# Four-layer cross-attention model: batches in pairs become a running sequence half the layers apart, and GpSimd adds two key tiles of probabilities before the sums

## Chip, cores and metric

One NeuronCore of one Trainium2 chip runs the whole program. The metric is the device time of the kernel in microseconds (us), as the median of several runs; lower is better. Engine names as the profile has them: PE is TensorE (PEld its weight loads), DVE is VectorE, ACT is ScalarE, POOL is GpSimd, SP is SyncE, which here only issues DMAs. PSUM is the memory that TensorE writes, SBUF the working memory.

## The reference, cut to what matters

The input is x (16 batches, 256 tokens, 128 channels) and a context ctx (16 batches, 1601 rows, 64 channels). Four layers follow each other, and each is an attention and a feed-forward part:

```python
x = x + L0_xattn(ln(x), ctx)   # causal self-attention + cross-attention, 16 heads of 8
x = x + L0_ffn(ln(x))          # top 4 of 32 hashed experts
x = x + L1_xattn(ln(x), ctx)   # cross-attention, 16 heads of 8
x = x + L1_ffn(ln(x))          # quantised, with a convolution over channels
x = x + L2_xattn(ln(x), ctx)   # self-attention, ffn, then cross-attention, ffn; 16 heads of 32
x = x + L2_ffn(ln(x))          # top 1 of 8 experts
x = x + L3_xattn(ln(x), ctx)   # cross-attention, 16 heads of 8
x = x + L3_ffn(ln(x))          # top 2 of 16 experts and a shared one
```

Batches are independent of each other. Within one batch every line needs the one above it. Each cross-attention is softmax(q k^T) v of 256 queries over 1601 keys in 16 heads. The "third attention" of the change is the cross-attention inside L2.

## The kernel before

**Work.** A cross-attention is cut into four *slabs* of four heads (`attend`, line 1046). A slab has two parts. First the maxima: 28 products of queries with stretches of keys into PSUM (tile `bank<-k,q`), each followed by a DVE reduction (`mx<-bank`). They give every query's largest score; POOL splits it in three bf16 parts (`thirds`, tile `nmp`), TensorE turns it (`shift_T`, tile `nmT`). Then seven steps over the 13 key tiles, two tiles a step and one in the last, which has 65 rows: transposed scores of four heads (`st_ops`, tiles `st<-q,k` and, for the subtracted maximum, `st<-nmT,ones`), four exponentials on ACT (`exps`, `p<-st`), and the products of probabilities with values and, for heads of 32, with a matrix of ones that gives the softmax's denominators (`weigh`, tiles `bank<-p,v` and `bank<-p,ones`). Four heads lie in four row or column groups of the array. Heads of 8 (L0, L1, L3; "narrow") carry the column of ones inside their values, so they have no products with ones. Heads of 32 (L2; "wide") use plain f32 operands, so a product of queries and keys is two matmul instructions and not one.

The rest of a batch is its *chain*: layer norms, projections, L0's and L2's self-attentions (`own_attention`), feed-forward parts, and for a new batch `load_ctx` (line 754), which loads and normalises the context and transposes it. `queries8`, `parts8` and `keys` for narrow heads spread the heads over the partitions with small DMAs on SP, four per slab (`spread`, line 808, tiles `q<-hl`, `k<-hl`): 16 for a batch's queries, 16 for its keys in each cross-attention, and 32 for L0's self-attention.

**Order.** Nothing is issued as it is written. `Program.record` (line 195) collects units of work, and `emit` (line 341) plans them: it keeps a clock for every engine, and whenever an engine is free takes the ready unit of lowest rank whose buffers are free. The plan's order is the program order of each engine on the chip. The rank is a level (`CHAIN` before `ENDS` before `OWN` before `STEPS`) and inside it a place. Chain work therefore goes first, L0's self-attention later, and the maxima and steps fill what is left, in the order of their places: step j of slab number n stands at n + j/7, its maxima at n - 1 - LEAD and up, with LEAD = 0.4 of a slab. A DMA of SP is planned at `t = 0.07` us of its queue (line 398). Matmuls of successive calls into one PSUM tile form one unit, so all products of a `weigh` are one.

**Buffers.** Each class of tiles has a number of places: 7 for `k` (the keys of a slab, also the context under load), 2 for `v`, 12 for `p`, 6 for `w4` (wide tiles: the queries of a cross-attention, the four tiles of a self-attention, hidden layers), 7 PSUM banks and one accumulator. `k`, `v` and the transposed contexts `ctxT` (2 places) are given out in the order of recording.

**Batches.** The loop at line 1365 takes two batches at a time. Per pair the order of cross-attentions is L0 of the first, L0 of the second, L1 of the first, L1 of the second, and so on. While one batch attends, the other one's chain runs. The context of the next pair is recorded after the whole of this pair.

Of the kernel before, what the change touches and what calls it, by code (L numbers as in the profile page):

```python
# [13 lines left out]
F32R = mybir.dt.float32r  # L14
# [3 lines left out]
ALU = mybir.AluOpType  # L18
# [3 lines left out]
P = 128  # L22
# [26 lines left out]

CHAIN, ENDS, OWN, STEPS = 0, 1, 2, 3  # L50

LEAD = 0.4
NAHEAD = 2


# [396 lines left out]
def model(ctx: ExitStack, tc: tile.TileContext, d, out):  # L452
# [158 lines left out]
    def places(tag, n, **how):  # L611
# [11 lines left out]
        for t, n, how in (  # L623
            ("bank", 7, {"psum": True}), ("acc", 1, {"psum": True, "gang": False}),
            ("k", 7, {"ordered": True}), ("v", 2, {"ordered": True}),
            ("ctxT0", LANES, {"ordered": True}), ("ctxT1", LANES, {"ordered": True}),
            ("p", 12, {}), ("wst", 2, {}), ("w4", 6, {}), ("tok", 10, {}), ("chan", 6, {}), ("chan_r", 3, {}),
            ("vs8", 1, {}), ("y8", 2, {}), ("nmT1", NAHEAD, {}), ("nmT4", 1, {}), ("nm4", 1, {}),
            ("lg32", 1, {}), ("lg8", 1, {}), ("lg17", 1, {}), ("gate32", 1, {}), ("gate8", 1, {}), ("gate17", 1, {}),
            ("bn", 4, {}), ("mv", 4, {}), ("rs", 4, {}), ("cm", 1, {}), ("cr", 1, {}), ("rc8", 4, {}), ("third", 4, {}),  # L630
            ("nm", 4, {}), ("mx", 4, {}), ("m8", 2, {}), ("ix", 2, {}), ("fx1", 2, {}), ("fx2", 2, {}), ("fx4", 2, {}),
            ("rw2", 2, {}), ("rw4", 2, {}), ("sw", 2, {}), ("am", 2, {}), ("sg", 1, {}),
        )
    }
    for tag, ts in (("nmp", nmp[4:]), ("nmp4", nmp[:4])):
# [6 lines left out]
    def new(tag, shape, base, dtype=F32, loose=False):  # L642
        return prog.tile(classes[tag], shape and list(shape), dtype, name(base), loose)
# [7 lines left out]
    def evac(o, i, bias=None):  # L651

        if bias is None:
            nc.scalar.copy(o, i)
        else:
            nc.scalar.activation(o, i, AF.Identity, bias=bias)
# [226 lines left out]
    def accumulators(tag):  # L883
        return bank(tag).rearrange("p (u q) -> p u q", u=2)

    def weigh(att, s, av, pr, t0, n, r, last, sums=True, values=True):


        for i in range(n):
            first, fin = t0 + i == 0, last and i == n - 1  # L890
            if values:
                for g in range(4):
                    mm(av[32 * g : 32 * g + 32, 0, :], att.value(s, t0 + i, g, r), pr[g][:r, i, :],
                       first and (sums or att.d8), fin, True)
            if sums and not att.d8:
                for g in range(4):
                    mm(av[32 * g : 32 * g + 32, 1, :], ones[:r, :32], pr[g][:r, i, :],
                       first and not values, fin, True)

    def normalised(att, s, av):  # L900
        if att.d8:
# [105 lines left out]
                    r = rows_of(t + whole)  # L1007
                    yield t + whole, 1, r, ps2[h][:r, whole * P : m * P]

    def keys(ctxT, l):  # L1010
        ks = {}
        if l == "l2":
            for s in range(4):
                t = new("k", [P, NK], "k32")
                for k0, k1, p in halves(wkv2[:, s * P : (s + 1) * P], ctxT[1], NK):
                    evac(t[:, k0:k1], p)
                ks[s] = t
        else:
            hl = [new("k", [P, NKE], "hl", F32R) for _ in range(2)]
            bias = W.get(l + "_bck")  # L1020
            for k0, k1, p in halves(W[l + "_Wck"], ctxT[0], NKE):
                split([t[:, k0:k1] for t in hl], p, bias)
            for s in range(4):
                t = new("k", [P, NKE], "k8", F32R, loose=True)
                spread(t, hl, s, True)
                ks[s] = t
        return ks

    def values(ctxT, l):
        vs = {}  # L1030
        if l == "l2":
            for s in range(4):
                v = new("v", [P, NT, P], "v32")
                for t, m, r, p in value_tiles(ctxT[1], wkv2[:, 512 + s * P : 512 + (s + 1) * P]):
                    evac(v[:r, t : t + m, :].rearrange("p t e -> p (t e)"), p)
                vs[s] = v
        else:
            v, v9 = values8("v", NT, ctxT[0])
            for t, m, r, p in value_tiles(ctxT[0], W[l + "_Wcv"]):
                evac(v9[:r, t : t + m, :, :8], p.rearrange("p (t h e) -> p t h e", t=m, h=H))  # L1040
            vs[0] = v
        return vs

    slab_no = [0]

    def attend(att):

        steps = [(t, min(2, NT - t), rows_of(t)) for t in range(0, NT, 2)]
        w = NKE if att.d8 else NK
        for s in range(4):  # L1050
            mx = new("mx", [P, 2, 4, 4], "mx", loose=True)
            stretches = [(range(q, q + 1), c * 512, c * 512 + 512) for q in range(2) for c in range(3)]
            stretches.append((range(2), 3 * 512, w))
            n = slab_no[0]
            slab_no[0] += 1
            for i, (qs, k0, k1) in enumerate(stretches):
                for g in range(4):
                    with prog.at(STEPS, n - 1 + (4 * i + g) / (4 * len(stretches)) - LEAD):
                        h = slice(32 * g, 32 * g + 32)
                        m, j = k1 - k0, k0 // 512  # L1060
                        p = bank()[:, : m * len(qs)].rearrange("p (q k) -> p q k", k=m)
                        with prog.together((g,)):
                            for q in qs:
                                mm(p[:, q - qs[0], :], att.q[h, s, q * P : (q + 1) * P], att.k[s][h, k0:k1])
                        nc.vector.tensor_reduce(mx[:, qs[0] : qs[-1] + 1, g, j], p, AX.X, ALU.max)
            with prog.at(ENDS):
                nm = new("nm", [P, 2, 4], "nm")
                nc.vector.tensor_reduce(nm, mx, AX.X, ALU.max, negate=True)
                sh = new("nmp", None, "nmp")
                thirds(sh, nm)  # L1070
                nmT = shift_T([sh])[:, 0, :]
            av = None
            for j, (t0, m, r) in enumerate(steps):
                with prog.at(STEPS, n + j / len(steps)):
                    pr = [exps(att, t, m, r) for t in st_ops(att, s, t0, m, r, nmT)]
                    if av is None:
                        av = accumulators("acc")
                    weigh(att, s, av, pr, t0, m, r, t0 + m == NT)
            with prog.at(ENDS):
                normalised(att, s, av)  # L1080
        return att.o


    def route(logits, n, k, gate):
# [277 lines left out]


    prog.recording = True
    for b0 in range(0, nb, LANES):
        lanes = range(b0, min(nb, b0 + LANES))
        ctxTs, lives = {}, {}
        for b in lanes:
            with prog.at(CHAIN):
                ctxTs[b] = load_ctx(b)  # L1370
                lives[b] = life(b, ctxTs[b])
        atts = {}
        for l in LAYERS:
            for b in lanes:
                with prog.at(CHAIN):
                    if l == "l0":
                        atts[b] = next(lives[b])
                with prog.at(CHAIN):
                    ks = keys(ctxTs[b], l)
                    vs = values(ctxTs[b], l)  # L1380
                atts[b].k, atts[b].v = ks, vs
                attend(atts[b])
                with prog.at(CHAIN):
                    atts[b] = next(lives[b], None)
    with tc.manual_schedule():
        prog.emit()

# [118 lines left out]
```

## Time and profile before

| what | value |
| --- | --- |
| median of 3 runs | 9560.31 us (9547.48 to 9571.74) |
| profiled execution: time, span | 9500.53 us, 9498.8 us |
| PE, DVE, ACT, POOL busy | 93%, 62%, 54%, 11% |
| mean granted TensorE clock | 0.904 |
| chain that ended last, by engine | PE 80%, DVE 8%, ACT 4%, SP's queue 3% |
| products with ones | 7680 instructions, 586.2 us busy |
| DMA | mean 33 GB/s |

The profile is of one execution, with its span counted from the first to the last instruction; its own time is 1.7 us longer. Busy time of PE counts matmuls that stand in its pipeline, so 93% doesn't say that it runs at its peak. The granted clock is a share of TensorE's full clock. All operations go through one helper, so they have one line (L395), and it is tiles that tell them apart.

### The profile page before, as it was taken

What the parts mean: (1) busy time and instruction counts of PE and PEld (TensorE: products, weight loads), DVE (VectorE), ACT (ScalarE), POOL (GpSimd) and SP (SyncE); (2) the same over time, 40 slices, a digit from 0 to 9 for tenths busy, and PEclk for the clock granted to TensorE, in tenths of its full rate; (3) what the DMA queues carried; (4) which work ended last, traced back from release to release, by engine and by line L of the source; (5) the groups of instructions that cost most, each with busy time, mean ns of one, the idle gap of its engine ahead of it and who ended that gap; (6) DMA issues with size and microseconds to landing.
All of it is one profiled execution on the core that took longest, in us unless ns stands there. A gap on an engine that the chain in (4) does not pass through costs nothing.

```text
span 9498.8 us, 210842 instructions
## 1 busy us (share of the span) xinstructions
PE 8874.5 (93%) x86118; PEld 5239.1 (55%) x86118; DVE 5863.8 (62%) x12308; ACT 5171.3 (54%) x10590; POOL 1080.9 (11%) x2747
## 2 busy tenths in 40 slices
PE   6999899998999989999899998999989999899999
PEld 3556555565555655556455564555645556455565
DVE  4755657556675565755667555676566755567555
ACT  2654556555564555645556454664555645566455
POOL 2011110111101011010110101101010010100100
PEclk7989889898898988989899897898988989899898
DMA  2200212002120021200212002120011101111011
GB/s 55 49 18 15 45 37 54 14 14 48 38 52 11 14 49 36 53 11 18 47 39 49 11 18 46 39 49 11 20 45 44 43 11 21 45 45 44 11 22 32
DMA packets 158879, 313.48 MB, mean 33 GB/s; under 512 B 65163, under 2 KB 116275, under 8 KB 157910
## 3 DMA queue, kind: packets, MB, share of 16 engines
q1 hardware_dynamic: 154676, 297.83, 13.6%
q8 instruction: 678, 11.11, 0.5%
q14 instruction: 291, 2.38, 0.1%
q0 software_dynamic: 768, 1.48, 0.0%
q10 hardware_dynamic: 2466, 0.68, 0.0%
HBM read 98.31 MB, written 2.10 MB: 11 GB/s over the span
## 4 chain that ended last, share of the span: by engine, by line
PE 80%; DVE 8%; ACT 4%; SPq 3%; issue 2%; DMA 2%; POOL 1%; ACTq 0%; DVEq 0%; POOLq 0%
PE bank L395 53%; PE st L395 22%; PE mx L395 4%; DVE mx L395 4%; SPq L395 3%; ACT p L395 3%; DMA k<-hl 1%; DVE z L395 1%; DVE x L395 1%; DVE st L395 1%; DMA ws<-in_s_l3f_dram 1%; DVE mv L395 0%; POOL nmp L395 0%; ACT ctxT L395 0%; DVE rc L395 0%
## 5 line engine op out<-in xcount | busy, mean ns | idle before, releaser
L395 DVE TENSOR_REDUCE mx<-bank 128x1 f32<-128x512 f32 (+2 forms) x7168 | 4093.1, 627 | 1967.6 <-PE bank L395 1871.6
L395 ACT ACTIVATE p<-st 128x512 f32<-128x512 f32 (+1 forms) x7680 | 3849.8, 575 | 2460.8 <-PE st L395 2310.6
L395 PE MATMUL st<-q,k 32*128 32x256 f32 (+1 forms) x18176 | 2531.6, 370 | 154.6 <-ACT p L395 105.7
L395 PE MATMUL bank<-k,q 32*128 32x512 f32 (+2 forms) x10240 | 2375.5, 521 | 174.8 <-DVE hl L395 88.6
L395 PEld LDWEIGHTS st<-q,k 32*128 32x128 f32 (+1 forms) x18176 | 1644.3, 190 | 1011.0 <-issue 361.7
L395 PE MATMUL bank<-p,v 128*32 128x256 f32 (+1 forms) x27648 | 2105.8, 412 | 0.0
L395 PE MATMUL st<-nmT,ones 32*128 32x512 bf16 (+1 forms) x7680 | 1682.0, 389 | 0.0
L395 PEld LDWEIGHTS bank<-k,q 32*128 32x128 f32 x10240 | 1042.2, 198 | 740.5 <-ACT p L395 199.5
L395 PEld LDWEIGHTS bank<-p,v 128*32 128x32 f32 (+1 forms) x27648 | 757.6, 114 | 896.6 <-issue 607.5
L395 POOL CAST nmp<-nm 128x8 bf16<-128x8 f32 x384 | 84.4, 220 | 4852.8 <-DVE nm L395 4465.1
L395 PE MATMUL bank<-p,ones 128*32 128x256 f32 (+1 forms) x7680 | 586.2, 384 | 0.0
L395 PEld LDWEIGHTS <-ones 32*128 32x128 bf16 (+1 forms) x7680 | 485.8, 98 | 116.5
L395 DVE TENSOR_REDUCE nm<-mx 128x2 f32<-128x512 f32 (+1 forms) x768 | 378.8, 520 | 253.8 <-PE mx L395 238.0
L395 DVE RECIPROCAL rc<-bank 128x8 f32<-128x8 f32 (+1 forms) x384 | 276.1, 719 | 293.0 <-PE bank L395 287.2
L395 POOL TENSOR_SCALAR_AFFINE_SELECT p<-p 128x512 f32<-128x512 f32 x512 | 300.3, 624 | 701.2 <-PE bank L395 490.0
L395 ACT ACT_TABLE_LOAD x222 | 284.8, 1283 | 149.5 <-PE st L395 108.0
L395 PE MATMUL mx<-k,q 32*128 32x256 f32 x1536 | 305.4, 426 | 63.0 <-DMA k<-hl 42.8
L395 POOL TENSOR_TENSOR rs<-rs,neghalf 128x2 f32<-128x2 f32 x240 | 170.3, 710 | 1663.3 <-DVE rs L395 1648.9
L395 PEld LDWEIGHTS bank<-p,ones 128*32 128x32 f32 (+1 forms) x7680 | 248.5, 111 | 178.0 <-issue 10.6
L395 ACT COPY v<-bank 128x512 f32<-128x512 f32 (+3 forms) x592 | 232.5, 451 | 144.5 <-PE bank L395 143.9
L395 PEld LDWEIGHTS mx<-k,q 32*128 32x128 f32 x1536 | 216.4, 215 | 164.5 <-issue 46.2
L395 PEld LDWEIGHTS bank<-ws,h 128*128 128x128 f32 x1664 | 231.7, 222 | 46.6 <-issue 32.3
(221 smaller groups left out, 6545.0 us busy)
## 6 DMA issues: line engine op xcount, KB each, us to landing
k<-hl SPq DMA_DIRECT2D x768, 200.2 KB, 3.6
q<-hl SPq DMA_DIRECT2D x1024, 32.0 KB, 1.9
ws<-in_s_l_a_li_dram SPq DMA_DIRECT2D x32, 768.0 KB
ws<-in_s_l3f_dram SPq DMA_DIRECT2D x32, 768.0 KB, 7.3
ws<-in_s_l0f_dram SPq DMA_DIRECT2D x32, 512.0 KB, 6.0
ws<-in_s_l_a_qkv_dram SPq DMA_DIRECT2D x16, 768.0 KB, 4.2
k<-hl SPq DMA_DIRECT2D x256, 32.0 KB, 1.9
ws<-in_s_l3f_dram SPq DMA_DIRECT2D x16, 384.0 KB
```

The source lines that it names most:

```text
L395: getattr(getattr(self.nc, e), method)(*a, **k)
```

## The change

**Batches.** The pairs go. One sequence of slabs for all 16 batches is made (`slabs_in_order`), and from the second batch on it repeats: L0 of batch b+1, L2 of batch b, L1 of batch b+1, L3 of batch b. Between L1 and L2 of one batch there now lie two cross-attentions of others (narrow ones), between its other layers one: L2's between L0 and L1, L1's between L2 and L3. A new batch's context is loaded when L3 of the batch two before it begins, and one at a time. The sequence starts with L0, L0, L1, L2 (of the first batch), L1 (of the second), L3 (of the first), and it ends with L1 and L3 of the last two and then L2 and L3 of the last batch alone.

**Places.** Steps and maxima get their places from a running count (`clock`): 18 units for a narrow slab, 34 for a wide one, 18 for a slab's maxima, which end 4 units ahead of its steps or earlier. The keys and values of a wide slab are recorded slab by slab, and a step now also waits for the values (`prog.behind`).

**Sums.** In a wide slab's six steps of two key tiles, POOL adds the two tiles' probabilities of each head (new tiles `ps`, four places), and TensorE multiplies that sum with ones, once and not twice. `p` has 11 places and not 12.

```diff
-LEAD = 0.4
+LONG8, LONG32, LONGM, LEAD = 18, 34, 18, 4
...
-            ("p", 12, {}), ("wst", 2, {}), ("w4", 6, {}), ...
+            ("p", 11, {}), ("wst", 2, {}), ("w4", 6, {}), ... ("ps", 4, {}),
...
-    def weigh(att, s, av, pr, t0, n, r, last, sums=True, values=True):
+    def weigh(att, s, av, pr, t0, n, r, last, sums=True, values=True, both=None):
...
-            if sums and not att.d8:
+            if sums and not att.d8 and both is None:
                 for g in range(4):
                     mm(av[32 * g : 32 * g + 32, 1, :], ones[:r, :32], pr[g][:r, i, :],
                        first and not values, fin, True)
+        if both is not None:
+            for g in range(4):
+                mm(av[32 * g : 32 * g + 32, 1, :], ones[:r, :32], both[g], False, last, True)
...
+    def attend(att, s, begin, ahead):
...
+                with prog.at(STEPS, ahead + (4 * i + g) * LONGM / (4 * len(chunks))):
...
+            with prog.at(STEPS, begin + j * (LONG8 if att.d8 else LONG32) / len(steps)), prog.behind(att.v[0 if att.d8 else s]):
...
+                both = None
+                if m == 2 and not att.d8:
+                    both = [new("ps", [P, T], "ps") for _ in range(4)]
+                    for o, e in zip(both, pr):
+                        nc.gpsimd.tensor_tensor(o, e[:, 0, :], e[:, 1, :], ALU.add)
+                weigh(att, s, av, pr, t0, m, r, t0 + m == NT, both=both)
...
+    def slabs_in_order():
+        def whole(b, l):
+            return [(b, l, s) for s in range(4)] if b < nb else []
+        seq = whole(0, "l0") + whole(1, "l0") + whole(0, "l1")
+        for b in range(nb):
+            x, y = whole(b, "l2"), whole(b + 1, "l0") if b else []
+            if y:
+                seq += y + x
+            else:
+                seq += x
+            seq += whole(b + 1, "l1") + whole(b, "l3")
+        return seq
+
+    def clock(seq):
+        begin, t = [], 0.0
+        for _, l, _ in seq:
+            begin.append(t)
+            t += LONG32 if l == "l2" else LONG8
+        ahead, t = [], 1e9
+        for t0 in reversed(begin):
+            t = min(t, t0 - LEAD) - LONGM
+            ahead.append(t)
+        return list(zip(seq, begin, reversed(ahead)))
...
-    for b0 in range(0, nb, LANES):
-        lanes = range(b0, min(nb, b0 + LANES))
...
+    begun(0)
+    begun(1)
+    for (b, l, s), begin, ahead in clock(slabs_in_order()):
+        att, ctxT = atts[b], ctxTs[b]
+        with prog.at(CHAIN):
+            if l == "l2":
+                att.k[s], att.v[s] = keys32(ctxT, s), val32(ctxT, s)
+            elif s == 0:
+                att.k, att.v[0] = keys8(ctxT, l), val8(ctxT, l)
+        if l == "l3" and s == 0:
+            begun(b + 2)
+        attend(att, s, begin, ahead)
+        if s == 3:
+            with prog.at(CHAIN):
+                atts[b] = next(lives[b], None)
```

`begun(b)` loads a batch's context, starts its chain and runs it up to L0's cross-attention; `keys8`, `val8`, `keys32` and `val32` are the two branches of the old `keys` and `values`.

## The prediction

> **What bounds the kernel now.** I read the page first.
>
> ```profile
> PE 8874.5 (93%) x86118; PEld 5239.1 (55%) x86118; DVE 5863.8 (62%) x12308; ACT 5171.3 (54%) x10590; POOL 1080.9 (11%) x2747
> PEclk7989889898898988989899897898988989899898
> PE 80%; DVE 8%; ACT 4%; SPq 3%; issue 2%; DMA 2%; POOL 1%; ACTq 0%; DVEq 0%; POOLq 0%
> L395 PE MATMUL bank<-p,ones 128*32 128x256 f32 (+1 forms) x7680 | 586.2, 384 | 0.0
> ```
>
> TensorE carries the end: 80% of the last chain, and no other engine near its limit. The clock row shows a dip in every fifth slice or so: a pair of batches lasts about 1180 us, five slices.
>
> So I looked at one pair. The last key tile's products have a form of their own (32x65), so the timeline tells when each slab ends. Cutting at the ends of attentions from 2527 us on gives eight stages: L0 twice, L1 twice, L2 twice, L3 twice (columns: length, then busy us of PE, PEld, DVE, ACT, POOL, then clock and DMA).
>
> ```profile
> 2527.00:2642.00 115.00, 110.55 (x1033) 65.91 (x1028) 79.13 (x165) 71.04 (x145) 4.99 (x20) 0.88 0.21 48
> 2642.00:2741.00 99.00, 94.40 (x998) 55.40 (x993) 77.10 (x165) 67.55 (x144) 6.44 (x22) 0.98 0.23 51
> 2741.00:2851.00 110.00, 105.97 (x1018) 61.17 (x1010) 75.31 (x162) 69.87 (x147) 6.42 (x22) 0.86 0.25 60
> 2851.00:2999.00 148.00, 142.35 (x1247) 80.07 (x1243) 82.10 (x177) 83.21 (x172) 21.18 (x53) 0.84 0.02 7
> 2999.00:3242.00 243.00, 231.08 (x2297) 142.39 (x2297) 138.94 (x286) 105.83 (x209) 28.69 (x69) 0.92 0.04 11
> 3242.00:3390.00 148.00, 146.37 (x1752) 91.31 (x1744) 84.73 (x170) 75.75 (x155) 7.92 (x24) 1.00 0.14 28
> 3390.00:3497.00 107.00, 100.94 (x1037) 59.30 (x1037) 80.98 (x175) 72.38 (x148) 19.73 (x33) 0.94 0.23 47
> 3497.00:3710.00 213.00, 183.79 (x1415) 103.31 (x1411) 113.12 (x238) 101.59 (x210) 37.24 (x96) 0.80 0.17 41
> ```
>
> Undisturbed slabs end 19.6 to 22.5 us apart when narrow (2699, 2719, 2741) and 33.8 us when wide. I take 20.5 and 34: 82 us for a narrow attention, 136 for a wide one. What the stages have over that is the price of the chains: 33, 17, 28, 66, 107, 12, 25, 131, together 419 of 1183 us. Two stages stand out. In the fifth the first wide slab ends only at 3133, 134 us after the stage begins: the first batch's chain of L1's feed-forward and L2's self-attention (from the last `o` at 2858 to the cross-attention's queries at 3020, 162 us) was not hidden by one narrow attention, and the second's then ran beside little else. In the eighth the next pair's two contexts and two L0 self-attentions fall together. There the plan is wrong about SP:
>
> ```profile
> 3521.49 10.75 SPq L395 DMA_DIRECT2D q<-hl  x16
> 3533.44 12.09 SPq L395 DMA_DIRECT2D q<-hl  x16
> 3545.63 10.10 SPq L395 DMA_DIRECT2D k<-hl  x16
> ```
>
> Sixteen small DMAs take 10.1 to 12.1 us to issue, 0.63 to 0.76 each where the plan has 0.07. TensorE, whose order is fixed, stands behind them:
>
> ```profile
> 3529.04 0.79 PE L395 MATMUL bank<-k,q 32*128 32x512 f32 x2 [9.98 <-DVE hl L395]
> 3542.05 1.22 PE L395 MATMUL bank<-zT,w_l_Wq 128*128 128x256 f32 x2 [3.87 <-DVE hl L395]
> 3553.31 0.76 PE L395 MATMUL mx<-k,q 32*128 32x256 f32 x2 [7.15 <-DMA k<-hl]
> ```
>
> That is 21 us of standing in a pair, and the clock after it is 0.50.
>
> **The change, part by part.** I sum against the profiled 9500.5 us, which lies 59.8 below the median of 9560.3.
>
> *Sums.* 64 wide slabs have six steps of two tiles; each loses four f32 products, eight instructions: 3072 of 7680. The timeline prices them in a wide slab:
>
> ```profile
> 3304.86 0.64 PE L395 MATMUL bank<-p,v 128*32 128x256 f32 x8
> 3305.32 0.61 PE L395 MATMUL bank<-p,ones 128*32 128x256 f32 x8
> 3305.75 0.61 PE L395 MATMUL bank<-p,v 128*32 128x256 f32 x8
> ```
>
> From start to start eight take 0.43 us, so 384 x 0.43 = 165 us. Bounds: nothing, if a wide slab waits for something else (its stage has PE busy 146 of 148 at full clock, which speaks against), and 3072 x 586.2/7680 = 234 by the group. I take -165.
>
> *GpSimd.* It gains 1536 additions of 128x256. The nearest row:
>
> ```profile
> L395 POOL TENSOR_TENSOR xb<-x,biases 128x256 f32<-128x256 f32 x96 | 69.7, 734 | 529.3 <-DVE x L395 528.7
> ```
>
> At 0.734 us that is 1127 us more of POOL (11% to about 23%), 2.9 per step of 34/7 = 4.9 us, so it fits beside the step. But the products of a step form one unit, which now waits for the last addition, with the next step's scores and the maxima behind it in TensorE's order, and ACT and DVE waiting for those. The cover is what the plan puts between, scores and maxima of later places, some 3 us a step in this stage; without it each of 384 steps stands for an addition, 384 x 0.734 = 282 us. `p` is held that much longer and has one place less: two steps take eight, so 11 still leave a third begun. And `thirds` (four operations of 0.22) may find an addition running: half of 0.734 at 64 slabs, 24 us. The lead of maxima before a wide slab shrinks from 0.4 of it to 4 of 34 units; later products fill what it opens. The new wait for values costs nothing: they are made a slab ahead. I take +25 for all this; bounds 0 and +282. One rule speaks against the additions: the Trainium skill (Advanced Engine Details and Errata, VectorE Performance Modes) has GpSimd share VectorE's second SBUF port, so that each blocks the other. The trace has 734 ns beside a VectorE mostly reducing from PSUM, and nothing on two-port instructions; were an addition to take twice that, four would need 5.9 us against 4.9, and the sum would be 384 us worse. I go by the row.
>
> *L1 to L2.* This chain now has two narrow attentions over it (164 us bare) and not one. The first batch's cost its stage 66 and the second's 107 over bare. If all cost 66: -41 for each of 8 pairs, -328. Bounds: 0 if 107 is work and not gaps; -66 more per pair if the first's cost halves for both.
>
> *New batch.* 131 in the eighth stage includes an L3 feed-forward, 33 in the first stage, so two loads cost 98, one 49. One at a time beside an L3 attention needs 32 small DMAs for itself and 16 for the queries at once, not 96. The stage lost 21 us of standing and, by clock 0.80, up to 0.2 x 213 = 43 more, 32 per batch. I take 0.6 of it, 19, for 14 batches: -266. Bounds: -32, and +49 (below). What the self-attention's own products do is unclear: the Trainium skill (TensorE: Matmul & The Clock Gate, Part 1) releases the clock after some 3.4 us of sustained activity, yet from 3560 to 3570 PE was busy 10.00 of 10 us at 0.50. By the rule nothing cold would remain beside an attention, and the term would be its full -448; I go by the row.
>
> *L2 to L3.* The first batch of a pair had this beside a wide attention at 12; now all pay 25 beside a narrow one: 13 x 8 = +104. L0's feed-forward goes from 17 and 28 beside narrow attentions to beside a wide one, where the sixth stage's chain cost 12: I take no change.
>
> *Ends.* The first batch's L1 to L2 has no attention over it: 162 - 66 = +96. The last batch's has one: +14. The last L2 to L3 stands open, 53 us (3396.5 to 3449.5) and 17 of maxima, less the 25 counted: +45. Together +155.
>
> Keys and values of wide slabs, recorded slab by slab, keep their cost and their queues; ACT copies and TensorE products are the same in number, and the place of `k` and `v` decided their time before too.
>
> Sum: -165 + 25 - 328 - 266 + 104 + 155 = -475, so 9025.5, and with 59.8 a median of 9085.
>
> **Rivals.**
> *Each load stalls alone (slower).* Place: SP's queue at every L3. The plan keeps 0.07 per DMA, so each batch can make TensorE stand as a pair did: a load costs 98 and not 30. Then +49 x 14 = +686 in the place of -266: 9978, median 10037. It decides from 64 us a load on (475/14 = 34 more than 30). For: the lines above. Against: only 21 of the 98 is standing, and one batch issues half.
> *Chains are work, not gaps (slower).* Neither -328 nor -266 comes: +119, 9619, median 9679. For: PE is busy 231 of 243 in the fifth stage. Against: that stage's 2297 instructions are fewer per us than the sixth's 1752 in 148.
> *The order does not come apart.* `w4` has six places: L3's queries 1, L2's self-attention 4, the new L0's queries 1, and then nothing for its own attention. If a batch waits for places, half of the 594 is lost: 9322, median 9382, faster by the sums and little else.
> *More hides.* With two attentions over it the chain from L1 to L2 costs all batches 33, half of 66: 528 more, less 66 at the two ends: 8563, median 8623.
>
> **Numbers.** Chances: forecast 0.50 (its own range 8900 to 9300), order not apart 0.15, more hides 0.13, loads stall 0.13, work not gaps 0.09. The range may leave out 0.2: the stalled loads and half of the last; 8600 to 9600. A measurement tells 0.3% (29 us) from no change. Faster: 0.50 + 0.15 + 0.13, less 0.02 of the second for no change and 0.01 for slower: 0.75. Slower: 0.13 + 0.09 + 0.01 = 0.23. No change: 0.02.
>
> **What would show it.** Right: `bank<-p,ones` with 4608 instructions; POOL near 2200 us with additions near 734 ns; no first wide slab over 100 us long after an L1, except the first batch's; narrow attentions with a chain beside them between 100 and 150 us, a steady cycle of four (382 bare, less 10 of sums, and chains of 33, 23, 25, 66 and 30) near 550 us and a mean clock over 0.92. Wrong: PE waits on `q<-hl` or `k<-hl` of 10 us and more at every L3, 14 times; wide steps ended by POOL rather than PE; or a clock at 0.90 as before.

## The result, and the profile after

The changed kernel takes 9687.1 us (median of 4 runs, 9630.3 to 9714.3) against 9553.9 us for the kernel before in the same comparison: ratio 1.0129, 95% interval 1.009 to 1.0168. It is slower by 1.3%, where 9085 and a range of 8600 to 9600 were predicted. The profiled execution took 9714.3 us, its span is 9712.6 us, 213.8 more than before's. It is the slowest of its four, and the one profiled before (9500.5) is faster than the median of its kernel; by the medians the two kernels lie 133 us apart.

The page of the changed kernel: busy time, the clock row and the last chain by engine.

```profile
PE 9017.9 (93%) x83046; PEld 5289.4 (54%) x83046; DVE 5891.6 (61%) x12308; ACT 5243.7 (54%) x10646; POOL 2147.8 (22%) x4283
...
PEclk6987898979889899897988989889897998988988
...
PE 79%; DVE 8%; SPq 4%; ACT 3%; issue 2%; DMA 1%; POOL 1%; ACTq 0%; DVEq 0%; POOLq 0%
```

GpSimd has doubled as predicted (2147.8 us, 22%). TensorE's row is full, its busy time is 143 us longer than before although it has 3072 instructions less, and the mean granted clock fell from 0.904 to 0.876. The groups of instructions show the part that was foreseen:

```profile
L397 POOL TENSOR_TENSOR ps<-p 128x256 f32<-128x256 f32 x1536 | 1076.1, 728 | 1076.1 <-PE bank L397 598.9 <-ACT p L397 473.3
...
L397 PE MATMUL bank<-ps,ones 128*32 128x256 f32 x3072 | 246.5, 389 | 0.1
...
L397 PE MATMUL bank<-p,ones 128*32 128x256 f32 (+1 forms) x1536 | 135.6, 462 | 0.0
```

1536 additions of 728 ns (734 predicted), 3072 + 1536 = 4608 products with ones. What waits for the additions is short; the largest such row in the list of waits (total us, times, longest) is ScalarE's next exponential waiting for a place of `p`:

```profile
ACT p L397 <- POOL ps L397: 170.3, 99, 2.6
```

One round of the new sequence, cut at the ends of attentions as before: L1, L3, L0, L2 (columns: length, busy us of PE, PEld, DVE, ACT, POOL, then clock and DMA).

```profile
3159.00:3264.00 105.00, 101.28 (x1024) 60.05 (x1024) 79.92 (x174) 69.05 (x141) 19.77 (x37) 0.90 0.22 43
3264.00:3480.00 216.00, 192.84 (x1550) 107.58 (x1542) 123.51 (x267) 106.14 (x214) 40.90 (x102) 0.81 0.15 38
3480.00:3601.00 121.00, 115.70 (x1077) 66.22 (x1078) 78.76 (x165) 77.61 (x157) 4.22 (x17) 0.94 0.04 12
3601.00:3749.00 148.00, 144.19 (x1555) 90.72 (x1548) 85.15 (x163) 75.96 (x158) 67.87 (x111) 0.95 0.16 34
```

About 590 us for a batch, where about 550 were predicted and a batch of before takes 588. The stage of L3 is the long one: 216 us, at a clock of 0.81. In it TensorE stands behind SP's queue, as the first rival said, once for every batch that is loaded (14 times, 9.9 to 13.2 us). SP issues the new batch's small DMAs one behind the other, here the last 32 of them, and TensorE's next product waits for the last:

```profile
3292.95 10.12 SPq L397 DMA_DIRECT2D q<-hl  x16
3303.17 10.09 SPq L397 DMA_DIRECT2D k<-hl  x16
```

```profile
3310.83 0.76 PE L397 MATMUL mx<-k,q 32*128 32x256 f32 x2 [13.01 <-DMA k<-hl]
3311.52 0.61 PE L397 MATMUL mx<-caus,ident 128*128 128x512 bf16 x1
```

All such waits together, from the list of waits (two of the 16 are at the start of the run):

```profile
PE mx L397 <- DMA k<-hl: 176.6, 16, 13.2
```

What comes after the standing runs slowly. The first of these stretches is the standing; in the next two TensorE is busy throughout, and the clock is still 0.50:

```profile
3304.00:3311.00 7.00, 0.17 (x1) 0.20 (x2) 0.00 (x0) 0.00 (x0) 0.00 (x0) 0.50 0.21 52
3311.00:3316.00 5.00, 5.00 (x13) 2.36 (x13) 2.13 (x4) 0.00 (x0) 0.00 (x0) 0.50 0.41 120
3316.00:3326.00 10.00, 10.00 (x27) 5.29 (x27) 9.22 (x19) 0.38 (x1) 0.00 (x0) 0.50 0.09 36
```

**Stages of all batches.** The clock's records hold only 1.00 and 0.50, so a stretch has a half-clock time of 2 x (1 - clock) x length. Its length less half of that is what it would take if all of it followed the clock and the clock were full; I call this its full-clock length. It is a reckoning and includes idle time. By the trace, as means over the twelve batches of the steady part (six pairs before), in us for one batch:

| kernel | length | half-clock time | full-clock length |
| --- | --- | --- | --- |
| before | 588.3 | 112.6 | 532.0 |
| after | 593.2 | 136.1 | 525.1 |
| of it in L0, L1, L2, L3: before | 108, 126, 194, 161 | 18, 24, 19, 52 | 99, 114, 185, 134 |
| after | 121, 107, 154, 212 | 14, 29, 13, 80 | 114, 92, 147, 172 |

The steady part is 4.9 us a batch longer: 6.9 shorter in full-clock length, and 23.5/2 = 11.8 longer by the clock. For 16 batches that is 78 us. The rest of the 214, 135 us, lies at the two ends, where attentions have no chain of another batch beside them. These are reckonings of one execution each; the means over all executions are given after number 16.

### The profile page after: what moved, and what is told of

Its sections match the earlier page's. It is cut to its first block, busy times and chain, and to the rows that moved or that the text cites. A ratio compares the mean times of both kernels' runs of the same rounds, so it can differ in the third digit from the quotient of the medians.

```text
span 9712.6 us, 207309 instructions
## 1 busy us (share of the span) xinstructions
PE 9017.9 (93%) x83046; PEld 5289.4 (54%) x83046; DVE 5891.6 (61%) x12308; ACT 5243.7 (54%) x10646; POOL 2147.8 (22%) x4283
## 4 chain that ended last, share of the span: by engine, by line
PE 79%; DVE 8%; SPq 4%; ACT 3%; issue 2%; DMA 1%; POOL 1%; ACTq 0%; DVEq 0%; POOLq 0%
PE bank L397 51%; PE st L397 24%; DVE mx L397 5%; PE mx L397 4%; SPq L397 4%; ACT p L397 3%; DMA k<-hl 1%; DVE z L397 1%; DVE rc L397 1%; DVE nm L397 0%; DVE hot L397 0%; ACT L397 0%; DVE st L397 0%; POOL nmp L397 0%; DVE hl L397 0%
## 5 line engine op out<-in xcount | busy, mean ns | idle before, releaser
L397 PE MATMUL st<-q,k 32*128 32x256 f32 (+1 forms) x18176 | 2635.0, 379 | 141.6 <-ACT p L397 96.1
L397 PE MATMUL bank<-k,q 32*128 32x512 f32 (+2 forms) x10240 | 2334.1, 521 | 111.4 <-DVE mx L397 34.0
L397 PEld LDWEIGHTS st<-q,k 32*128 32x128 f32 (+1 forms) x18176 | 1769.6, 197 | 993.8 <-issue 348.7
L397 PE MATMUL st<-nmT,ones 32*128 32x512 bf16 (+1 forms) x7680 | 1817.1, 399 | 0.0
L397 PEld LDWEIGHTS bank<-k,q 32*128 32x128 f32 x10240 | 1017.1, 197 | 716.8 <-issue 233.7
L397 POOL TENSOR_TENSOR ps<-p 128x256 f32<-128x256 f32 x1536 | 1076.1, 728 | 1076.1 <-PE bank L397 598.9
L397 PEld LDWEIGHTS <-ones 32*128 32x128 bf16 (+1 forms) x7680 | 522.4, 100 | 133.0 <-issue 4.7
L397 DVE TENSOR_TENSOR h<-bank,h 128x512 f32<-128x512 f32 x224 | 154.5, 690 | 332.7 <-PE bank L397 317.3
L397 ACT CAST nmT<-bank 128x256 bf16<-128x256 f32 (+1 forms) x320 | 132.4, 414 | 367.4 <-PE bank L397 365.0
```

What stands on the lines that cost most here:

```text
L397: getattr(getattr(self.nc, e), method)(*a, **k)
```

## The experiments

Ratios are to the kernel before in the same comparison, with their 95% interval; "steady" is the length of a batch as in the table.

**1. The order without the sums.** From the changed kernel, with `p` at 12 places and no `ps`:

```diff
-                if m == 2 and not att.d8:
+                if False:
```

> The changed order alone: GpSimd adds nothing, p has its 12 places again and every key tile has its own products with ones. If the sums are worth the 165 us of the forecast, this is about 9850 us, 165 above the changed kernel's 9687, and the order alone costs 300. If the additions only replace one wait by another (probabilities held longer, ACT waiting for their places), it is 9690 or below.

Measured: 9967.1 us, ratio 1.0436 (1.0356 to 1.0516). One round of it, L3, L0, L2, L1:

```profile
5757.00:5974.00 217.00, 192.09 (x1540) 109.98 (x1542) 123.13 (x266) 105.83 (x213) 40.12 (x101) 0.83 0.15 38
5974.00:6088.00 114.00, 109.79 (x1067) 63.82 (x1066) 79.52 (x165) 76.02 (x153) 4.19 (x17) 0.97 0.04 13
6088.00:6249.00 161.00, 157.57 (x1776) 98.67 (x1768) 82.52 (x161) 76.85 (x160) 6.39 (x22) 0.94 0.15 32
6249.00:6367.00 118.00, 108.62 (x1017) 62.76 (x1016) 80.97 (x177) 69.24 (x142) 15.21 (x29) 0.85 0.19 38
```

The order costs 436 us by the medians, more than the 300 of the expectation. Steady 611.3: half-clock time 144.5, full-clock length 539.0. The stages are 218 us (L3), 112, 164 and 117 in the mean, against 212, 121, 154 and 106 with the sums: the sums shorten L2 and L1, and the L3 stage is long without them too. Half-clock time in the L3 stage is 83 us, where a batch of before has 52; that is nearly all of the 32 us of half-clock time that the order adds, since the other three stages together add 1.

**2. The sums without the order.** The kernel before, with `ps`, `both` and `behind` as in the change, `p` at 11 places, and the four additions of a step in one unit.

> The sums alone in the kernel of before: pairs of batches and their places as before, GpSimd's additions, p 11 and ps 4, the four additions of a step recorded as one unit and a step waiting for its values (so that the plan can go on). By the forecast's row 165 us faster: about 9390. If TensorE only waits for the additions instead: 9500 to 9560. Together with the run of the order alone it tells whether the two parts add up.

Measured: 9567.0, ratio 1.0021 (0.9985 to 1.0056): no change can be told. The two wide stages of a pair:

```profile
3009.00:3248.00 239.00, 224.27 (x2000) 134.32 (x2000) 139.54 (x281) 96.67 (x195) 90.52 (x159) 0.91 0.03 10
3248.00:3396.00 148.00, 145.43 (x1579) 92.10 (x1575) 86.62 (x169) 77.35 (x157) 75.36 (x123) 0.97 0.14 28
```

They were 243 and 148; in the mean of the six pairs the two together were 388.0 and are 390.3. The products with ones went from 7680 instructions to 4608 here too, but the second stage runs at 0.97 where it ran at 1.00. Over a pair's steady part the full-clock length fell by 2.9 us a batch, and half-clock time rose by 13.1. So the sums bring nothing in the old order and 280 us in the new one (9967 to 9687 by the medians): the two parts of the change don't add.

**3 and 4. SP's queue planned as it runs.** In the changed kernel and in the kernel before:

```diff
-                    t = 0.07
+                    t = 0.65
```

> The changed kernel, planned with 0.65 us for each DMA of SP's queue in place of 0.07; the operations are the same, only the order of issue changes. Theory A, each load stalls alone: TensorE stands 13 us behind k<-hl once per batch and runs at half clock for some 60 us after it; a plan that knows the queue puts other work there, 30 to 40 us per batch, so 9100 to 9250. Theory B, the chains of L1 to L2 and of the new batch are TensorE work that now falls together beside L3: at most the standing goes, 13 x 15 = 200, so 9480 to 9690.

> The kernel of before with the same 0.65 us in its plan. Theory A: a pair stands 21 us and runs at half clock for 50 us after it: 7 x 45 = 315 faster, about 9240. Theory B: at most 7 x 21 = 150, about 9400 or above. Beside the changed kernel with 0.65 it tells whether the new order loses more to the plan's ignorance of SP than the old one.

Measured: in the changed kernel 9724.0, ratio 1.016 (1.0084 to 1.0236); in the kernel before 9421.6, ratio 0.9836 (0.9763 to 0.9908). The last chain, first of the changed kernel with this edit, then of the kernel before with it:

```profile
PE 83%; DVE 9%; ACT 4%; issue 2%; POOL 1%; SPq 0%; DMA 0%; ACTq 0%; POOLq 0%; DVEq 0%
```

```profile
PE 84%; DVE 9%; ACT 3%; issue 2%; POOL 1%; SPq 1%; DMA 0%; ACTq 0%; POOLq 0%; DVEq 0%
```

SP's queue is nearly gone from the last chain in both (4% and 3% without the edit). In the old order that is worth 1.6%; in the new one it brings nothing: the L3 stage stays (212 and 214 us in the mean), and its half-clock time rises from 80 to 92 us. So taking away the standing that is seen at every load of the changed kernel was not enough to win its time back; the edit changes the order of everything else too, so it doesn't give the standing's own price.

**5. A longer lead of the maxima** (changed kernel, `LEAD` 12 and not 4).

> The changed kernel with maxima that end 12 units ahead of their slab's steps and not 4 (before: 7.2 units of a narrow slab, 13.6 of a wide one). In the changed kernel's trace a wide slab's last maximum comes as the slab before it ends, and its first exponential 10 to 15 us later. Theory lead: this costs 1 to 2 us at each of 256 slabs, so 9180 to 9430. Theory chains: TensorE does later maxima meanwhile and nothing is lost, 9640 to 9730.

Measured: 9835.6, ratio 1.0311 (1.0275 to 1.0347). Longer lead, longer time: a longer lead doesn't win back what the order costs. Its full-clock length fell (521.7), its half-clock time rose to 165.0.

**6 and 7. Without L0's self-attention**, in both orders.

```diff
         with prog.at(OWN):
-            qs = queries8("l0_Wq", "l0_bq", zT)
...
-            own = own_attention(att, True, (ALU.is_ge, -1))
...
-        nc.vector.tensor_tensor(oth, oth, own, ALU.add)
```

> The changed kernel without L0's self-attention (its projections, 32 small DMAs, products, and the addition of its output are left out). Theory chains-are-work: the price of one is the same in both orders, 16 times what it costs the kernel of before, some 25 to 30 each: 9210 to 9290. Theory falling-together: beside L3 it meets the chain of L1 to L2, each makes the other dearer, and it costs 40 to 50: 8890 to 9050.

> The kernel of before without L0's self-attention, the pair to the run above. The stage with two of them stands 98 us over bare and feed-forward; about half of that is the context: 25 to 30 for each self-attention, so 9050 to 9130 in both theories. It is the price that the changed kernel's is held against.

Measured: 9155.5 in the new order, ratio 0.9596 (0.9561 to 0.9631), and 8943.4 in the old, 0.9391 (0.9351 to 0.943), below the 9050 to 9130 that were expected. The steady length falls by 29.0 us in the new order and 34.9 in the old. One load at a time makes this part a little cheaper, and the new order is still the slower one by 212 us. An L3 stage of the new order without this part, and a second L3 stage of a pair in the old order without it:

```profile
3047.00:3228.00 181.00, 169.87 (x1317) 93.76 (x1313) 109.59 (x239) 92.15 (x184) 27.23 (x67) 0.77 0.16 40
```

```profile
3291.00:3421.00 130.00, 115.09 (x1044) 69.16 (x1041) 85.72 (x185) 77.23 (x158) 9.65 (x27) 0.87 0.21 51
```

In the old order half-clock time in that stage falls from 85 to 30 us in the mean. In the new one, where no load brings its standing or its self-attention any more, it stays: 80 and 86. So this part is not what alone keeps the clock of the new L3 stage low.

**8. L2's self-attention spread over the attentions beside it** (changed kernel: its parts get places among the steps, from 18 + 36 units behind the start of L1's last slab, 12 units apart).

> The changed kernel with L2's self-attention ranked among the steps, at places that run from the third slab of the L3 beside it into the following L0, and no longer ahead of all steps. Theory falling-together: the L3 stage loses some 40 of its 134 us over bare and the L0 stage takes 20 to 30 of it with a warmer clock: 9300 to 9500. Theory chains-are-work: only the place moves, 9600 to 9750.

Measured: 9756.2, ratio 1.0233 (1.0197 to 1.0269). The L3 stage falls from 212 to 190 us and the stage of L0 rises from 121 to 138; steady 595.1. The time only moves from one stage to the next, as time that TensorE needs would.

**9. Products added in the standing** (changed kernel; `ident16` by `caus`, a full 128x128 product, overwritten at once).

```diff
                 with prog.together(None if causal else (g,)):
+                    if causal and s == 0 and g == 0:
+                        for _ in range(24):
+                            mm(sc, ident16, caus, True, True)
```

> The changed kernel with 24 more products (128x128 by 128x512, bf16, overwritten at once) ahead of the first score of L0's self-attention, where TensorE stands 13 us for the keys of the new batch at every L3 and then runs the self-attention at a granted clock of 0.50 (0.64 over 3300 to 3376). At half clock a product of this form goes every 0.43 us or so (0.61 busy), at full clock half of that, so the 24 take 5 to 10 us and lie inside the standing. If the order's price is a colder array (the clock follows how much of the array was used lately), work added in the standing brings the clock back for the self-attention: of its roughly 66 us at 0.64 some 10 to 20 come off per load, 140 to 280 us in all, 9400 to 9550, and the stage of L3 shows a clock above 0.88. If the price is TensorE's work and the clock only goes along with it, nothing is gained and some of the added products show: 9690 to 9800, with the clock of that stage still near 0.81 after the added products. If the standing sets the pace, no change within 0.5%.

Measured: 9696.6, ratio 1.0128 (1.0085 to 1.0171). In the profiled executions half-clock time falls by 202 us, half of that is 101, and the added products cost 85 in full-clock length (by the means of all executions 47 and 61): the time does not move.

**10 and 11. Without L2's self-attention**, in both orders.

```diff
-            yT = affine_T(pz, pre + "_lny_g", pre + "_lny_b", "yT")
...
-            own_attention(att, False, (ALU.is_gt, 1))
-        o = att.o
+        o = att.o if cross else slabs(w[:, :512], xT, "q")
```

> The changed kernel without L2's self-attention and its key and value projections (the queries go on in the place of its result). It is the longest part of the chain from L1 to L2. If chains cost what TensorE needs for them, whichever attention lies over them, it is worth the same here as in the kernel before with the same part left out, 25 to 45 us a batch, 400 to 700 us in all: 9000 to 9290, still 130 to 290 us above the kernel before with the same edit. If the prediction's gaps are the price (half of the chains of before unhidden, all of them hidden here), it is worth clearly less here than there, and the distance grows over 300. If the new order makes this part dearer, it is worth 100 us more here than there and the distance falls under 120.

> The kernel before without L2's self-attention and its key and value projections, to stand beside the changed kernel with the same edit. By additive work 400 to 700 us off, 8850 to 9150, and the stages of the first and of the second wide attention of a pair (66 and 107 over the bare ones) fall by about the same total as the same number of batches of the changed kernel. By gaps the fall sits in the stage where the first wide slab ends 134 us after its start: that slab comes down to 60 us or less and the rest stays.

Measured: 9117.8 in the new order, ratio 0.9548 (0.9505 to 0.9591), and 8857.5 in the old, 0.9254 (0.9209 to 0.9299). This is the test of the prediction's largest term. The old order's stages that held 66 and 107 over the bare ones, without this part:

```profile
2690.00:2823.00 133.00, 126.25 (x1090) 68.02 (x1092) 86.65 (x204) 79.15 (x162) 12.12 (x29) 0.90 0.04 13
2823.00:2995.00 172.00, 170.61 (x1886) 101.54 (x1883) 97.84 (x213) 85.58 (x173) 12.05 (x29) 1.00 0.03 11
```

148 comes to 133 and 243 to 172; by the means of all pairs 147.3 to 128.9 and 239.4 to 170.3. So 18 of the 66 and 69 of the 107 are this one part, which the pair's two batches do once each. In the new order it is the L3 stage, 212 to 176.5 in the mean:

```profile
2486.00:2667.00 181.00, 161.05 (x1248) 90.52 (x1246) 104.50 (x242) 93.77 (x190) 27.94 (x70) 0.79 0.18 45
```

By batch the part costs 41.7 us in the old order (30.7 of it full-clock length) and 38.7 in the new (28.7). A second attention over the chain saves 3 us a batch of this part by the steady lengths (8 by all executions, below), where 20.5 were predicted for the chain. In the old order the fall sits mostly in the stage of the first wide slab, which ends 52.5 us after its start now, as the expectation had it for gaps. But TensorE's idle time in the two stages only goes from 17.8 to 7.8 us a pair: of the 87 us that leave, it was busy in 77. The distance between the orders, 130 to 290 expected for additive work and over 300 for gaps, came out at 260.

**12 and 13. More products, and without a standing.** Number 9 with 56 products, and 24 of them in the kernel before with 0.65 us for SP.

> The changed kernel with 56 added products ahead of L0's self-attention and not 24. With 24 they ran at full clock in 5.35 us, 5.10 us of standing were left after them, and from the end of that standing the clock was 0.50 again; the stage of L3 kept its 212 us, with 70 us at half clock and not 80. 56 need 12 us at full clock, as long as the standing of 13. If the clock after the standing is what the stage pays, the score products now run at full clock, a pair in some 0.65 us and not 1.26: 10 us off for the 16 pairs of each load and more from what follows them, the stage of L3 at 190 to 202 us, its time at half clock under 45, in all 9400 to 9550. If half clock comes from the little that the chain's own products use of the array, the clock falls again within the self-attention, and the added products only take the place of the standing: 9660 to 9780, with 60 us or more at half clock in each L3.

> The kernel before with 0.65 us planned for each DMA of SP (9421.6 alone) and 24 added products ahead of each L0 self-attention. The standing is gone there, so the added products have nothing to fill and can only act through the clock. If they keep it up, the last stage of a pair (182.5 us, 58.6 of them at half clock) comes to 165 or so and the total to 9280 to 9350. If the clock falls within the self-attention whatever goes ahead of it, they cost 24 times 0.21 to 0.43 us for each of 16 loads, 80 to 165: 9480 to 9590.

Measured: 56 in the changed kernel, 9543.9, ratio 0.9983 (0.9955 to 1.0011): work was added and 143 us went away. In the other, 9492.9, ratio 0.9941 (0.9911 to 0.997), 71 more than without them, as expected if the clock falls anyway: the last stage of a pair goes from 182.5 to 193 us, with 59 us at half clock in both. The first one's timeline and clock about the added products:

```profile
3235.68 12.26 PE L397 MATMUL mx<-caus,ident 128*128 128x512 bf16 x56
3249.77 0.47 PE L397 MATMUL mx<-k,q 32*128 32x256 f32 x2 [1.83 <-DMA k<-hl]
```

```profile
3235.00:3249.00 14.00, 12.94 (x58) 5.41 (x56) 5.46 (x13) 0.60 (x1) 0.00 (x0) 1.00 0.20 52
3250.00:3253.00 3.00, 3.00 (x15) 1.72 (x14) 1.85 (x3) 0.59 (x1) 0.00 (x0) 0.93 0.19 51
3253.00:3262.00 9.00, 9.00 (x32) 6.56 (x32) 3.26 (x6) 0.58 (x1) 0.00 (x0) 0.50 0.26 89
```

The standing is filled (1.83 us are left of 13) at full clock, and the score products begin at 0.93; but 3 us on the clock is 0.50 again, with TensorE busy. The L3 stage loses 2.5 us only, against 10 to 22 expected, and the stage of L0 9. The planner had counted the added products, so this order is not the changed kernel's. Hence the next two.

**14 and 15. That order alone, and those products alone.** Number 14 has the order of the run with 56 products and doesn't issue them; number 15 has the changed kernel's order, instruction for instruction, and issues them.

> The order of the run with 56 added products, without these products: the planner still counts their time, so all other instructions stand as they stood there, and the 896 products are not issued. If that run (9543.9, with 1932 us at half clock and not 2407) was faster for its clock, this order alone is no better than the changed kernel: 9640 to 9730, the time at half clock over 2300 us and the standing of 13 us at each load back. If it was faster because the longer unit made the planner set the rest in a better order, this one is as fast or faster: 9480 to 9550.

> The changed kernel's own order, instruction for instruction, with the 56 added products issued ahead of each L0 self-attention and not counted by the planner. By the clock: 9520 to 9600, time at half clock under 2050 us. By the planner's order: 9690 to 9780, since nothing but added work has changed.

Measured, with the half-clock time of the profiled run and, in brackets behind it, the mean of all executions:

| order | without the products | with the 56 products |
| --- | --- | --- |
| of the change | 1.0129 (1.009 to 1.0168), 2407 us (2304) | 1.0171 (1.013 to 1.0212), 2188 us (2118) |
| with the products counted | 1.0050 (1.0026 to 1.0074), 2311 us (2212) | 0.9983 (0.9955 to 1.0011), 1932 us (1932) |

The order alone takes 0.8% off, with the standing still there (list of waits: total us, times, longest):

```profile
PE mx L399 <- DMA k<-hl: 172.1, 15, 13.2
```

The products alone give nothing: by the means of all executions they save 93 us of clock (half of 186) and cost 105 of full-clock length. In the other order they save 140 and cost 103, and the intervals of 1.0050 and 0.9983 lie apart. So by the ratios the order that came with the products is about one half of the gain of number 12 and the clock the other, and the clock's half is only had in that order.

**16. Sums and SP's time together in the old order.**

> The kernel before with GpSimd's sums and with 0.65 us planned for each DMA of SP. Alone the sums gave +36 (interval around no change) and the planned time -109 to -150. If the sums' work is saved in any order and only the clock took it back in the old one (525 of 588 us of a batch at full clock came to 529 with the sums, with 13 us more at half clock), the two add up to 9390 to 9460 and the time at half clock rises by 100 us or more over the 1995 us without the sums. If the sums are worth their 165 to 280 us once TensorE no longer stands, 9150 to 9290. If the additions hold up the steps, over 9500 with steps ended by GpSimd.

Measured: 9426.1, ratio 0.9864 (0.9799 to 0.9928). Half-clock time is 1864 us in the profiled execution, the fastest of its four; their mean is 1996, against 1935 without the sums. The sums still bring nothing that the intervals could tell. No version of the new order beats the kernel before; of the kernels with the whole computation, the kernel before with SP's queue planned at 0.65 us has the lowest median, 9421.6, and this one cannot be told from it.

**All executions together.** Each execution has its span and its mean granted clock (to three decimals) on record, so full-clock length and half-clock time can be reckoned for every one and not for the profiled one alone. Means, in us for a whole run:

| kernel | executions | full-clock length | half-clock time |
| --- | --- | --- | --- |
| before | 56 | 8573 | 1941 |
| the order alone | 4 | 8700 | 2543 |
| the sums alone | 10 | 8532 | 2062 |
| the change | 4 | 8526 | 2304 |
| without L0's self-attention, old order | 4 | 8152 | 1588 |
| the same, new order | 4 | 8024 | 2272 |
| without L2's self-attention, old order | 4 | 8079 | 1550 |
| the same, new order | 4 | 8045 | 2153 |

The order costs 127 us of full-clock length and 301 by the clock (half of 602). The sums take 174 us of length and 120 of clock off the new order; in the old one they take off 41 of length, and the clock takes 60 back. Leaving out L2's self-attention saves nearly the same length in either order, 494 us in the old and 481 in the new, but 196 by the clock in the old and 76 in the new. For L0's it is 421 and 502 of length, and 177 and 16 by the clock.

## Why the prediction was wrong

It was a sum of sound parts and of two terms that failed, L1 to L2 (-328) and the new batch (-266). The order was to gain 335 us with its ends and cost 436. Both failed terms took time in which TensorE was busy, in part at half clock, for time that another order would hide or win back. The second rival, "chains are work, not gaps", named that, and I gave it 0.09. That its 9679 lies 8 us from the measured 9687 is luck: it has the order at +259 (155 and 104) and the sums with their additions at -140, where 436 and -280 were measured, and the two errors nearly cancel.

**Ends: right.** +155 predicted, 135 measured by the two profiled executions, whose distance from the medians (214 against 133) leaves that open by some 80. The places are those that were named: the first batch's L2 stage lasts 280 us, 144 over bare, where 162 was assumed, and the last L3 stage 144 us, 62 over bare, where 70 was assumed. Outside the twelve steady batches the full-clock length is the same to 7 us, and half-clock time rose by 297 us.

**GpSimd: right.** 728 ns against 734, beside VectorE's 5891.6 us; POOL 2147.8 against 2200. The rule that was weighed against it, the Trainium skill's sharing of VectorE's second port (Advanced Engine Details and Errata, VectorE Performance Modes), shows in no row here: the additions are no longer than the earlier ones, and VectorE's busy time rose by 28 us of 5864. Waits for the additions sum to 170 us on ScalarE, which is not the bound. What the +25 for such waits came to was not measured by itself.

**Sums: the size depends on the order.** -165 predicted; in the new order -280 by the medians, by all executions 174 of full-clock length, about the size that was worked out, and 120 of clock, which the prediction had not counted. In the old order, from whose trace the price was taken, +36 by the medians, not to be told from nothing: the length fell by 41 only and the clock took 60 back. So "its stage has PE busy 146 of 148 at full clock, which speaks against" did not hold there: that stage fell from 1.00 to 0.97 with the products gone. Why the length falls by 41 in one order and by 174 in the other stays open.

**L1 to L2: failed, the largest term.** The step that failed is "The first batch's cost its stage 66 and the second's 107 over bare. If all cost 66: -41". It took two stages for two batches: the first chain ended at 3020, 21 us after the stage cut at 2999, so its end was in the 107. And it took the 107 for gaps: TensorE was idle for 12 us in that stage and 6 in the one before. PE's 231 of 243 busy, which stood in the rival, was the sign. With L2's self-attention taken out, 18 and 69 leave the two stages, 87 for two batches, against 35.5 for one in the new order's L3 stage, so at most 8 us a batch, 131 in all, came of this part and not 328; by all executions it is 133, and all but 13 of that is clock. What was foreseen of the place did come: in the steady part the first wide slab ends 40.7 us after its stage begins, where it took 129 or more in the first batch of a pair. But the time went into the L3 stage, 212 us long. The rest of the chain, L1's feed-forward above all, was not taken out by itself.

**New batch: failed.** 49 per load was to fall to 30, of which most by the clock: "up to 0.2 x 213 = 43 more, 32 per batch. I take 0.6". Measured, the standing is 11.6 us per load in the mean where it was half of 21, and half-clock time in the L3 stages rose from 52.3 to 80.2 us a batch, worth 14 the wrong way. That the loads bring it is not shown: without L0's self-attention and its standing the stage has 86 us. What the runs do show is the price of that self-attention, 29.0 us a batch in the new order and 34.9 in the old, so 6 saved where 19 were predicted for each load as a whole. The context's part of a load was not taken out. The first rival had the standing at every L3, but at the length of before, and so no further 49 per load from it.

**What stays open.** The order costs 436 us; 127 of it is full-clock length and 301 clock. The steady part has 23.0 us a batch of it, 7 in length and 16 by the clock ((144.5 - 112.6)/2), and the clock's part lies in the L3 stage, where the chain of one batch and the load of the next now fall together. But with either of the two self-attentions left out this stage keeps 86 or 68 us at half clock of 80, so neither alone is the cause, and no run left out both. The removals show what did not come, 594 us of gain; they don't show what made the order dearer than before. Numbers 14 and 15 add that a small change of the order is worth 0.8%, and that products in the standing gain in one of two orders; which places make the clock fall was not separated.

**The signs that were named.** Products with ones, POOL's time and the additions' length: as predicted. No first wide slab over 100 us but the first batch's: as predicted, 177 there, 72 in the last batch and 40.7 in all others. Narrow attentions with a chain within 150 us: not so, 212. A clock over 0.92 and a cycle near 550: 0.876 and 593. Of the signs for wrong, PE's waits on `k<-hl` of 10 us and more came at 13 of the 14 loads, and 9.9 us at the other; a plan without them gave nothing (number 3), so they marked the place and weren't shown to be the price.

## What to carry to other kernels

Before a chain's price is counted as a gap to be hidden, look at how long TensorE is idle in its stage, here 18 us of 173 over bare, and take a part of the chain out in one run of each order: L2's self-attention cost nearly the same full-clock length in both. A stage is not a batch; cut prices where a chain ends and not where the attention beside it ends. And where the granted clock changes with the load, a saved product is worth its time only if the clock holds: look at length and half-clock time side by side, over several executions, since either can give back what the other took.

## What the hardware showed that I had not expected

Full-clock length is steadier than time. Over 56 executions of the kernel before it lies between 8551 and 8595 us, while half-clock time goes from 1783 to 2137. Over the profiled executions of the kernels with the whole computation and no added products it lies between 8431 and 8718 us, while spans run from 9363 to 9937; half-clock time goes from 1828 to 2760 us.

TensorE can be busy without a gap and stay at 0.50: 10.00 of 10 us from 3316 on in the changed kernel, and again within 3 us of 56 full products at full clock. The Trainium skill (TensorE: Matmul & The Clock Gate, Part 1) lets one busy window of about 3.4 us release the clock; these stretches, in which pairs of 32-row products alternate with one full 128x512 product, are busy for longer by the profile and don't release it, so for them the measurement decides. What the gate counts was not measured by itself here.
